# Two-axis attention block on one core: output products moved next to the projections, and one sum product in the time attention

## The chip, the cores and the metric

The kernel runs on one core of one Trainium2 chip. The metric is the device time of one launch in microseconds (us). The core has five engines with a queue each: PE (TensorE, matrix products into PSUM), ACT (ScalarE), DVE (VectorE), POOL (GpSimd) and SP (SyncE, which issues the large DMAs here). Each takes its instructions in the program's order; waits between engines go over semaphores.

## The reference

The input x is [2, 256, 128, 128] in f32: batch, time, frequency band, channel. Three residual blocks follow each other:

```
x = x + attention over time(layernorm(x))    # 4 heads of 32, causal, for each batch and band: 256 steps
x = x + attention over bands(layernorm(x))   # 4 heads of 32, |i - j| <= 16, for each batch and time: 128 bands
x = x + w2(gelu(w1(layernorm(x))))           # 128 -> 512 -> 128
```

Each attention is softmax(q k / sqrt(32) + mask) v, followed by an output projection. All of it is computed in f32.

## The kernel before

The kernel first folds scales and biases into the weights (`fold`), tests on the chip that the scores are bounded, and then takes `bounded_path`: since scores are bounded, softmax needs no maximum, so the weights are just exp of the scores, and masks set weights to zero afterwards.

The work is cut into groups of 4 tiles of 128 tokens x 128 channels. 128 `OverTime` groups come first (one group: two bands of 256 steps); their result goes to DRAM. Then 16 runs follow, each of 8 `OverBands` groups (4 time steps of 128 bands each) and the 8 `FeedForward` groups on the same tokens.

A group goes through these methods; each names what it puts on which engine:

- `statistics` (DVE), `root` (POOL: two instructions on rstd), `normalize` (DVE: xh), `transpose` (PE: xp), `take_transposed` (copies xp to xnT; DVE for `OverTime`, ACT for the others);
- `queries_keys` and `values` (PE: qp, kp, vp), `take_query` (ACT: qT), `take_key` (kT: DVE for `OverTime`, ACT for `OverBands`), `take_values` (ACT: v);
- scores (PE: sp) in `first_half` and, for `OverTime`, `second_half`; exp on ACT in `first_function` and `second_function` (pt, or pf for bands); masks in `first_mask` and `second_mask` (POOL; the last head or two of a band group on DVE, a product with `band`);
- `weigh` (PE: rp, the sums of the weights, each a product with ones; and op, the weights with v), `invert` (ACT: ln, then exp(-ln), r), `divide` (DVE: t, u, oT, where t reads rp and u reads op);
- `output` (PE: yp) and `finish` (DVE: adds yp to the residual; for `OverTime` two store DMAs on SP). `bias` (POOL) prepares the residual tile with the output bias (rd for time, x for bands, res for the feed-forward).

For `FeedForward` the two halves are the hidden products hp with their gelu (hT), `weigh` is the product zp, and `divide` adds and stores.

In the time attention a group's weights lie in a tile pt of [128, 2 sequences s, 4 heads, blocks of 128]. The keys are on the partitions. Block 0 holds the first 128 keys for the first 128 queries, block 1 the first keys for the second queries, block 2 the second keys for the second queries. POOL masks blocks 0 and 2 (the diagonal ones). The sum for the first queries is over block 0, the sum for the second over blocks 1 and 2, so `weigh` has two sum products for each head: one of 512 columns over blocks 0 and 1 of both sequences, one of 256 over block 2, which is added in PSUM.

What each product uses of PE's array stands in the profile's rows: sp uses 32 rows (a head's channels are contracted), rp and op use 32 columns (a head's channels come out), all others the whole 128 by 128.

All PSUM tiles are one bank in size and come from one pool of 8 (`bank`), in turn: a tile waits until the readers of the one eight before it are done. In SBUF, pt and pf share a tag with three buffers.

The order on each engine is that in which `run` calls the methods: a step n handles group n's scores while n - 1 is weighed, n - 2 is put out and n + 1 to n + 3 are prepared. `InOrder` pins each instruction to this order. `feeds[i]` and `bands[i]` tell whether group n - 2 + i is a `FeedForward` or an `OverBands`; an `OverTime` group is neither. As all instructions are recorded in that helper, the profile gives nearly all of them its line, L812 (L821 with the change), and they are told apart by their tiles.

Of the kernel before, what the change touches and what calls it, by code (L numbers as in the profile page):

```python
# [18 lines left out]
P = 128  # L19
H = 4  # L20
# [404 lines left out]
class Group:  # L425
# [48 lines left out]
    def take_transposed(self):  # L474
        path = self.path
        self.xnT = path.work.tile([P, NT * P], F32, name="xnT")
        if isinstance(self, OverTime):
            path.vector.tensor_copy(self.xnT, self.xp)
        else:
            path.scalar.copy(self.xnT, self.xp)  # L480

    def first_half(self):
        pass
# [13 lines left out]
    def second_mask(self):  # L497
        pass
# [16 lines left out]
    def weigh(self):  # L515
        pass
# [89 lines left out]
def rows_of(h):  # L606
    return slice(h * D, (h + 1) * D)


class OverTime(Attention):  # L610

    which = 0
# [22 lines left out]
    def weights(self, s):  # L637
        path = self.path
        for h in range(H):
            path.scalar.activation(self.p[:, s, h, :], self.sp[h], AF.Exp)  # L640

    def mask(self, s):
        path = self.path
        for n in (0, 2):
            blk = self.p[:, s, :, n * P : (n + 1) * P]
            path.gpsimd.affine_select(
                out=blk, in_=blk, compare_op=ALU.is_ge, fill=path.zero, base=0,
                pattern=[[0, H], [1, P]], channel_multiplier=-1,
            )

    def first_half(self):
        self.p = self.path.work.tile([P, 2, H, self.W], F32, name="pt", tag="p")
        self.scores(0)
# [4 lines left out]
    def first_mask(self):  # L658
        self.mask(0)

# [8 lines left out]

    def weigh(self):  # L670
# [3 lines left out]
        one = path.k.ones[:, 0:D]  # L674
        for h in range(H):
            path.tensor.matmul(rp[rows_of(h), :, :], one, p[:, :, h, 0 : 2 * P], start=True, stop=False)
        for h in range(H):
            path.tensor.matmul(rp[rows_of(h), :, P : 2 * P], one, p[:, :, h, 2 * P : W], start=False, stop=True)
# [14 lines left out]
class OverBands(Attention):  # L693
# [39 lines left out]
    def first_half(self):  # L733
        self.p = self.path.work.tile([P, H, NT, P], F32, name="pf", tag="p")
        self.scores(range(H))
# [81 lines left out]
class BoundedPath:  # L817
# [79 lines left out]
    def run(self, x, out):  # L897
# [7 lines left out]
        def at(n, kind):  # L905
            return 0 <= n < len(groups) and isinstance(groups[n], kind)

        self.scalar.preload_act_table_set(EXP_SET)
        for n in range(-10, len(groups) + 2):
# [7 lines left out]
            if feeds[1]:  # L917
                if bands[0]:
                    do(n - 2, "output", "finish")
                do(n - 1, "weigh", "divide")  # L920
            elif feeds[2]:
                do(n - 1, "weigh", "invert", "divide")
            else:
                do(n - 2, "output", "finish")
            if feeds[3]:
                do(n + 1, "transpose", "take_transposed")
            do(n + 2, "normalize")
            do(n + 3, "root")
            if not bands[2]:
                do(n, "bias")  # L930
                if at(n + RUN // NT, OverBands):
                    do(n + RUN // NT, "bias")
            if bands[2]:
                do(n, "second_mask")
            if not feeds[1] and not feeds[2]:
                do(n - 1, "weigh", "invert", "divide")
            do(n, "second_half", "second_function")
            if not bands[2]:
                do(n, "second_mask")
            if feeds[2] and bands[1]:  # L940
                do(n - 2, "output", "finish")
            do(n + 1, "queries_keys", "take_query", "take_key", "values", "take_values")
            if at(n + 2, Attention):
                do(n + 2, "transpose", "take_transposed")
# [69 lines left out]
```

## Time and profile before

| | before |
|---|---|
| time, median of 3 runs | 3059.23 us (3058.98 to 3059.82) |
| profiled execution: its time | 3059.68 us |
| profiled execution: span from the first to the last instruction | 3057.8 us |
| busy, PE / DVE / ACT / POOL | 99% / 68% / 64% / 58% of the span |
| matrix passes on PE | 31270 |
| first time step's scores on PE | 33.6 us from the start |
| first feed-forward product | 1210.9 us from the start |

In a row of the timeline stand start and length in us, engine, line, operation, output tile, operands, shape and how many were merged; in brackets the idle time before and who ended it. On PE the pair ahead of the shape (32*128) is rows times columns of the array. A length on PE is modelled and overlaps the next product's, so what a product costs is read from start to start. A row of the groups has count, busy time, mean length in ns, idle time ahead. A row of the waits has the total, the count and the longest.

### The profile page before, as it was taken

Reading aid. Unit: us, or ns where it says so; the run is one execution under the profiler, and the core shown is the slowest. Engines: PE = TensorE matmul, PEld = TensorE weight load, DVE = VectorE, ACT = ScalarE, POOL = GpSimd, SP = SyncE. Lnnn points to the kernel's source line nnn. Section 1 sums busy time; section 2 is a strip of 40 time slices with the busy share of each in tenths; the row PEclk is TensorE's granted clock in tenths of the full one; section 3 lists DMA queues with packets and bytes.
Section 4 is the critical chain, followed back from the end, with each engine's and each line's share of the span. In section 5 each row is a group of like instructions: output and inputs, shape, how many; then the busy total and the mean of one; then the engine's idle time right before and its main releaser. Section 6 shows DMA issues by size and latency. Waiting matters only on the chain.

```text
span 3057.8 us, 77275 instructions
## 1 busy us (share of the span) xinstructions
PE 3027.1 (99%) x31270; PEld 2134.0 (70%) x31270; DVE 2090.3 (68%) x6206; ACT 1960.3 (64%) x3536; POOL 1787.2 (58%) x2409
## 2 busy tenths in 40 slices
PE   7999999999999999999999999999999999999999
PEld 5666666666666666777777767777767767777776
DVE  6888788788888888467476475575575674664763
ACT  4666666666666667567566576576575675675664
POOL 3555555555555576566566566565565665665662
PEclk9999999999999999999999999999999999999999
DMA  3222222222222221111101011111111111011001
GB/s 83 60 60 57 65 69 58 59 60 60 70 61 60 57 60 54 42 32 40 43 29 43 29 39 38 34 39 36 36 39 39 32 40 42 29 43 39 15 19 29
DMA packets 222863, 140.53 MB, mean 46 GB/s; under 512 B 7968, under 2 KB 205984, under 8 KB 222496
## 3 DMA queue, kind: packets, MB, share of 16 engines
q1 hardware_dynamic: 221248, 134.45, 15.4%
q8 instruction: 247, 4.05, 0.5%
q10 hardware_dynamic: 1248, 1.05, 0.1%
q14 instruction: 120, 0.98, 0.1%
HBM read 68.36 MB, written 67.11 MB: 44 GB/s over the span
## 4 chain that ended last, share of the span: by engine, by line
PE 95%; DVE 3%; ACT 2%; DMA 0%; POOL 0%; issue 0%; SPq 0%; ACTq 0%; POOLq 0%; DVEq 0%
PE zp L812 15%; PE hp L812 13%; PE sp L812 12%; PE rp L812 9%; PE qp L812 9%; PE yp L812 8%; PE op L812 8%; PE vp L812 7%; PE kp L812 7%; PE xp L812 5%; DVE xh L812 1%; ACT L812 1%; DVE pf L812 0%; ACT r L812 0%; DVE stats L812 0%; ACT ln L812 0%
## 5 line engine op out<-in xcount | busy, mean ns | idle before, releaser
L812 POOL TENSOR_SCALAR_AFFINE_SELECT pf<-pf 128x512 f32<-128x512 f32 x736 | 499.0, 693 | 309.6 <-ACT pf L812 284.5
L812 POOL TENSOR_SCALAR_AFFINE_SELECT pt<-pt 128x512 f32<-128x512 f32 x512 | 313.5, 635 | 469.7 <-ACT pt L812 469.7
L812 ACT ACTIVATE pt<-sp 128x384 f32<-128x384 f32 x1024 | 419.5, 497 | 204.4 <-PE sp L812 204.4
L812 PEld LDWEIGHTS zp<-w2T_sb,hT 128*128 128x128 f32 x4096 | 475.2, 192 | 48.4 <-issue 46.3
L812 DVE TENSOR_TENSOR res<-zp,res 128x512 f32<-128x512 f32 x128 | 88.6, 692 | 583.8 <-POOL x L812 330.7
L812 PE MATMUL zp<-w2T_sb,hT 128*128 128x128 f32 x4096 | 479.9, 276 | 0.1
L812 PE MATMUL hp<-xnT,w1f 128*128 128x512 f32 x1024 | 471.8, 596 | 7.0 <-ACT xnT L812 7.0
L812 ACT ACTIVATE hT<-hp,b 128x512 f32<-128x512 f32 x512 | 344.8, 687 | 138.3 <-PE hp L812 135.9
L812 POOL TENSOR_TENSOR rstd<-rstd,mhalf 128x4 f32<-128x4 f32 x384 | 407.5, 1061 | 32.0
L812 PE MATMUL sp<-qT,kT 32*128 32x128 f32 (+1 forms) x8192 | 389.5, 315 | 0.0
L812 PEld LDWEIGHTS sp<-qT,kT 32*128 32x128 f32 x8192 | 311.1, 185 | 72.7 <-issue 40.4
L812 PEld LDWEIGHTS vp<-wf,xnT 128*128 128x128 f32 x2048 | 269.9, 192 | 122.8 <-issue 115.2
L812 ACT COPY xnT<-xp 128x512 f32<-128x512 f32 x256 | 150.5, 588 | 317.4 <-PE xp L812 317.4
L812 POOL TENSOR_SCALAR rstd<-mv 128x4 f32<-128x4 f32 x384 | 93.6, 244 | 410.6 <-DVE mv L812 410.6
L812 PEld LDWEIGHTS hp<-xnT,w1f 128*128 128x128 f32 x1024 | 181.0, 190 | 174.2 <-issue 134.5
L812 ACT ACTIVATE pf<-sp 128x512 f32<-128x512 f32 x512 | 264.3, 603 | 57.9 <-PE sp L812 50.4
L812 PE MATMUL yp<-wn,oT 128*128 128x128 f32 x2048 | 293.3, 286 | 0.0
L812 PE MATMUL qp<-xnT,wf 128*128 128x512 f32 x512 | 286.1, 641 | 0.8 <-DVE xnT L812 0.8
L812 PEld LDWEIGHTS yp<-wn,oT 128*128 128x128 f32 x2048 | 250.1, 191 | 42.7 <-PE hp L812 11.9
L812 PE MATMUL vp<-wf,xnT 128*128 128x128 f32 x2048 | 270.8, 276 | 0.0
L812 PE MATMUL kp<-xnT,wf 128*128 128x512 f32 x512 | 262.5, 594 | 0.0
L812 PE MATMUL xp<-ident,xh 128*128 128x128 f32 x1536 | 232.2, 274 | 10.1 <-DVE xh L812 10.1
(93 smaller groups left out, 4801.2 us busy)
## 6 DMA issues: line engine op xcount, KB each, us to landing
xt<-in_x SPq DMA_DIRECT2D x64, 512.0 KB, 5.1
x<-rd SPq DMA_DIRECT2D x256, 128.0 KB, 1.9
out<-res SPq DMA_DIRECT2D x128, 256.0 KB, 2.3
xb<-x SPq DMA_DIRECT2D x32, 0.5 KB, 6.1
w1T_sb<-in_w1T ACTq DMA_DIRECT2D x1, 256.0 KB, 4.0
w2T_sb<-in_w2T ACTq DMA_DIRECT2D x1, 256.0 KB, 4.4
t_wiT_sb<-in_t_wiT ACTq DMA_DIRECT2D x1, 192.0 KB, 2.5
f_wiT_sb<-in_f_wiT ACTq DMA_DIRECT2D x1, 192.0 KB, 3.8
```

Source lines behind the costliest of these rows:

```text
L812: return self.tc.keep_in_program_order(emit(*args, **kwargs))
```

## The change

It has four parts.

1. **One sum product in the time attention.** pt gets a fourth block for each sequence and head. Block 3 is blocks 1 + 2, added by POOL for the first sequence (behind the first masks) and by DVE for the second (a new method `last_sum`, at the end of the step). The sum product then reads blocks 0 and 3 of both sequences, 512 columns in four stretches of 128; the second sum product of each head is gone. op's products stay. Block 2 is masked ahead of block 0.
2. **Buffers.** pt and pf have two buffers instead of three.
3. **xnT on ACT.** `take_transposed` copies on ACT for all groups.
4. **The order of `run`.** `output` and `finish` move behind `weigh` (bands) or behind `second_half` (time), so that yp stands directly ahead of qp. Masks, `bias`, `normalize`, `root` and the transpose of the feed-forward groups move as shown.

```diff
--- before.py
+++ after.py
@@ -474,10 +474,7 @@
     def take_transposed(self):
         path = self.path
         self.xnT = path.work.tile([P, NT * P], F32, name="xnT")
-        if isinstance(self, OverTime):
-            path.vector.tensor_copy(self.xnT, self.xp)
-        else:
-            path.scalar.copy(self.xnT, self.xp)
+        path.scalar.copy(self.xnT, self.xp)

     def first_half(self):
         pass
@@ -495,6 +492,9 @@
         pass

     def second_mask(self):
+        pass
+
+    def last_sum(self):
         pass

     def queries_keys(self):
@@ -637,19 +638,25 @@
     def weights(self, s):
         path = self.path
         for h in range(H):
-            path.scalar.activation(self.p[:, s, h, :], self.sp[h], AF.Exp)
+            path.scalar.activation(self.p[:, s, h, 0 : self.W], self.sp[h], AF.Exp)

     def mask(self, s):
         path = self.path
-        for n in (0, 2):
-            blk = self.p[:, s, :, n * P : (n + 1) * P]
+        for n in (2, 0):
+            blk = self.block(s, n)
             path.gpsimd.affine_select(
                 out=blk, in_=blk, compare_op=ALU.is_ge, fill=path.zero, base=0,
                 pattern=[[0, H], [1, P]], channel_multiplier=-1,
             )

+    def block(self, s, n):
+        return self.p[:, s, :, n * P : (n + 1) * P]
+
+    def add(self, engine, s):
+        engine.tensor_tensor(self.block(s, 3), self.block(s, 1), self.block(s, 2), ALU.add)
+
     def first_half(self):
-        self.p = self.path.work.tile([P, 2, H, self.W], F32, name="pt", tag="p")
+        self.p = self.path.work.tile([P, 2, H, self.W + P], F32, name="pt", tag="p", bufs=2)
         self.scores(0)

     def first_function(self):
@@ -657,6 +664,7 @@

     def first_mask(self):
         self.mask(0)
+        self.add(self.path.gpsimd, 0)

     def second_half(self):
         self.scores(1)
@@ -667,15 +675,16 @@
     def second_mask(self):
         self.mask(1)

+    def last_sum(self):
+        self.add(self.path.vector, 1)
+
     def weigh(self):
         path = self.path
         p, v, W = self.p, self.v, self.W
         rp = path.bank([P, 2, 2 * P], "rp")
-        one = path.k.ones[:, 0:D]
+        sums = p.rearrange("p s h (n q) -> p s h n q", q=P)[:, :, :, 0:4:3, :]
         for h in range(H):
-            path.tensor.matmul(rp[rows_of(h), :, :], one, p[:, :, h, 0 : 2 * P], start=True, stop=False)
-        for h in range(H):
-            path.tensor.matmul(rp[rows_of(h), :, P : 2 * P], one, p[:, :, h, 2 * P : W], start=False, stop=True)
+            path.tensor.matmul(rp[rows_of(h), :, :], path.k.ones[:, 0:D], sums[:, :, h], start=True, stop=True)
         op = path.bank([P, 2, 2 * P], "op")
         for s in range(2):
             for h in range(H):
@@ -731,7 +740,7 @@
         path.scalar.copy(self.kT, self.kp)

     def first_half(self):
-        self.p = self.path.work.tile([P, H, NT, P], F32, name="pf", tag="p")
+        self.p = self.path.work.tile([P, H, NT, P], F32, name="pf", tag="p", bufs=2)
         self.scores(range(H))

     def weigh(self):
@@ -914,32 +923,28 @@
             if bands[2] and feeds[1]:
                 self.scalar.preload_act_table_set(EXP_SET)
             do(n, "first_half", "first_function", "first_mask")
-            if feeds[1]:
-                if bands[0]:
-                    do(n - 2, "output", "finish")
-                do(n - 1, "weigh", "divide")
-            elif feeds[2]:
-                do(n - 1, "weigh", "invert", "divide")
-            else:
-                do(n - 2, "output", "finish")
-            if feeds[3]:
-                do(n + 1, "transpose", "take_transposed")
             do(n + 2, "normalize")
             do(n + 3, "root")
+            if bands[2]:
+                do(n, "second_mask")
+            if feeds[2] and feeds[3]:
+                do(n + 1, "transpose", "take_transposed")
+            do(n - 1, "weigh")
+            if not feeds[1]:
+                do(n - 1, "invert")
+            if bands[2]:
+                do(n - 2, "output", "finish")
+            do(n - 1, "divide")
+            if feeds[3] and not feeds[2]:
+                do(n + 1, "transpose", "take_transposed")
+            do(n, "second_half", "second_function")
             if not bands[2]:
-                do(n, "bias")
+                do(n, "second_mask", "bias")
                 if at(n + RUN // NT, OverBands):
                     do(n + RUN // NT, "bias")
-            if bands[2]:
-                do(n, "second_mask")
-            if not feeds[1] and not feeds[2]:
-                do(n - 1, "weigh", "invert", "divide")
-            do(n, "second_half", "second_function")
-            if not bands[2]:
-                do(n, "second_mask")
-            if feeds[2] and bands[1]:
                 do(n - 2, "output", "finish")
             do(n + 1, "queries_keys", "take_query", "take_key", "values", "take_values")
+            do(n, "last_sum")
             if at(n + 2, Attention):
                 do(n + 2, "transpose", "take_transposed")
```

What this does to PE in the time stage, from a step's first scores to its query projection (sp are scores, yp the output product, rp sums, op weights with v, qp the projection; kp, vp and xp follow it in both). Before:

```order
L812 MATMUL sp<-qT,kT 128x256 x4
L812 MATMUL sp<-qT,kT 128x128 x4
L812 MATMUL yp<-wn_106,oT 128x128 x4
L812 MATMUL rp<-pt,ones 32x512 x4
L812 MATMUL rp<-pt,ones 32x2x128 x4
L812 MATMUL op<-pt,v 32x256 x4
L812 MATMUL op<-pt,v 32x128 x4
L812 MATMUL op<-pt,v 32x256 x4
L812 MATMUL op<-pt,v 32x128 x4
L812 MATMUL sp<-qT,kT 128x256 x4
L812 MATMUL sp<-qT,kT 128x128 x4
L812 MATMUL qp<-xnT,wf_103 128x512
```

With the change:

```order
L821 MATMUL sp<-qT,kT 128x256 x4
L821 MATMUL sp<-qT,kT 128x128 x4
L821 MATMUL rp<-pt,ones 32x512 x4
L821 MATMUL op<-pt,v 32x256 x4
L821 MATMUL op<-pt,v 32x128 x4
L821 MATMUL op<-pt,v 32x256 x4
L821 MATMUL op<-pt,v 32x128 x4
L821 MATMUL sp<-qT,kT 128x256 x4
L821 MATMUL sp<-qT,kT 128x128 x4
L821 MATMUL yp<-wn_106,oT 128x128 x4
L821 MATMUL qp<-xnT,wf_103 128x512
```

The product yp went from between sp and rp to between the step's second sp and qp, and the second row of rp is gone.

DVE in a step of the time stage, before (t, u and oT are the division, xh the normalized tile):

```order
L812 COPY xnT<-xp 128x512
L812 BN_STATS stats<-xt 128x6 x4
L812 BN_AGGR mv<-stats 128x2 x4
L812 TENSOR_TENSOR rd<-yp,rd 128x512
L812 TENSOR_SCALAR xh<-xt,mv,rstd 128x128 x4
L812 TENSOR_TENSOR t<-rp,r_14821 128x512
L812 TENSOR_TENSOR u<-op,r_14821 128x512
L812 SCALAR_TENSOR_TENSOR oT<-t,u 128x512
L812 COPY kT<-kp 128x512
```

With the change:

```order
L821 TENSOR_TENSOR pt<-pt 128x4x128
L821 BN_STATS stats<-xt 128x6 x4
L821 BN_AGGR mv<-stats 128x2 x4
L821 TENSOR_SCALAR xh<-xt,mv,rstd 128x128 x4
L821 TENSOR_TENSOR t<-rp,r_14702 128x512
L821 TENSOR_TENSOR u<-op,r_14702 128x512
L821 SCALAR_TENSOR_TENSOR oT<-t,u 128x512
L821 TENSOR_TENSOR rd<-yp,rd 128x512
L821 COPY kT<-kp 128x512
```

The copy of xnT is gone, the add on pt has come behind kT's copy, and rd<-yp has moved from ahead of xh to behind oT.

POOL in a step of the time stage, before and then with the change (the x4 are the second half's two masks and the next step's first two):

```order
L812 AFFINE_SELECT pt<-pt 128x4x128 x4
L812 TENSOR_SCALAR rstd<-mv 128x4
L812 TENSOR_TENSOR rstd<-rstd,mhalf 128x4
L812 TENSOR_TENSOR rd<-xt,orow_112 128x512
L812 AFFINE_SELECT pt<-pt 128x4x128 x4
```

```order
L821 AFFINE_SELECT pt<-pt 128x4x128 x2
L821 TENSOR_TENSOR pt<-pt 128x4x128
L821 TENSOR_SCALAR rstd<-mv 128x4
L821 TENSOR_TENSOR rstd<-rstd,mhalf 128x4
L821 AFFINE_SELECT pt<-pt 128x4x128 x2
L821 TENSOR_TENSOR rd<-xt,orow_112 128x512
```

The add on pt stands ahead of rstd, and rd's add has moved from between rstd and the second half's masks to behind them.

PE at the start of the feed-forward groups of a run, before (the first hp belongs to the first of them):

```order
L812 MATMUL sp<-qT,kT 128x128 x16
L812 MATMUL yp<-wn_146,oT 128x128 x4
L812 MATMUL xp<-ident,xh 128x128 x4
L812 MATMUL rp<-pf,ones 32x512 x4
L812 MATMUL op<-pf,v 32x128 x16
L812 MATMUL hp<-xnT,w1f 128x512 x2
L812 MATMUL rp<-pf,ones 32x512 x4
L812 MATMUL op<-pf,v 32x128 x16
L812 MATMUL xp<-ident,xh 128x128 x4
L812 MATMUL hp<-xnT,w1f 128x512 x2
L812 MATMUL yp<-wn_146,oT 128x128 x4
L812 MATMUL hp<-xnT,w1f 128x512 x2
```

With the change:

```order
L821 MATMUL sp<-qT,kT 128x128 x16
L821 MATMUL rp<-pf,ones 32x512 x4
L821 MATMUL op<-pf,v 32x128 x16
L821 MATMUL yp<-wn_146,oT 128x128 x4
L821 MATMUL xp<-ident,xh 128x128 x4
L821 MATMUL hp<-xnT,w1f 128x512 x2
L821 MATMUL xp<-ident,xh 128x128 x4
L821 MATMUL rp<-pf,ones 32x512 x4
L821 MATMUL op<-pf,v 32x128 x16
L821 MATMUL hp<-xnT,w1f 128x512 x2
L821 MATMUL yp<-wn_146,oT 128x128 x4
L821 MATMUL hp<-xnT,w1f 128x512 x2
```

The first xp is now directly ahead of its hp, and the second xp stands ahead of rp and not behind the second op.

## Prediction

> **What bounds the kernel now.** I read the page first, for its busy shares and its chain, then the list of waits, for those on PE.
>
> ```profile
> PE 3027.1 (99%) x31270; PEld 2134.0 (70%) x31270; DVE 2090.3 (68%) x6206; ACT 1960.3 (64%) x3536; POOL 1787.2 (58%) x2409
> ...
> PE 95%; DVE 3%; ACT 2%; DMA 0%; POOL 0%; issue 0%; SPq 0%; ACTq 0%; POOLq 0%; DVEq 0%
> ```
>
> ```profile
> PE hp L812 <- ACT xnT L812: 7.0, 16, 0.5
> ...
> PE rp L812 <- POOL pt L812: 1.3, 1, 1.3
> ```
>
> PE is the bound: it is 95% of the chain that ends last, and in the steady part it waits for another engine only 16 times (the first row of waits, once in each run of 8 band groups and 8 feed-forward groups). So what leaves PE's queue leaves the time, unless another engine takes its place. A busy PE says nothing of what a product costs, since products overlap; the starts do. Here is one step of the time stage on PE (start, length, product; the multiplicity is twice that of the code, as each f32 product shows as two passes):
>
> ```profile
> 803.36 0.94 PE L812 MATMUL sp<-qT,kT 32*128 32x256 f32 x16
> 804.22 1.16 PE L812 MATMUL yp<-wn,oT 128*128 128x128 f32 x8
> 805.31 1.50 PE L812 MATMUL rp<-pt,ones 128*32 128x512 f32 x16
> 806.62 1.48 PE L812 MATMUL op<-pt,v 128*32 128x256 f32 x32
> 808.04 0.94 PE L812 MATMUL sp<-qT,kT 32*128 32x256 f32 x16
> 808.90 1.13 PE L812 MATMUL qp<-xnT,wf 128*128 128x512 f32 x2
> 809.86 1.02 PE L812 MATMUL kp<-xnT,wf 128*128 128x512 f32 x2
> 810.72 1.05 PE L812 MATMUL vp<-wf,xnT 128*128 128x128 f32 x8
> 811.61 0.60 PE L812 MATMUL xp<-ident,xh 128*128 128x128 f32 x4
> 812.14 0.50 PE L812 MATMUL sp<-qT,kT 32*128 32x256 f32 x4
> ```
>
> From start to start a step takes 812.14 - 803.36 = 8.78 us, without a gap. The pair behind PE is the part of the array used: sp uses 32 rows, rp and op 32 columns, the others all of it. The same products with other neighbours:
>
> ```profile
> 1807.28 1.88 PE L812 MATMUL hp<-xnT,w1f 128*128 128x512 f32 x4
> 1808.99 1.05 PE L812 MATMUL yp<-wn,oT 128*128 128x128 f32 x8
> 1810.47 1.99 PE L812 MATMUL hp<-xnT,w1f 128*128 128x512 f32 x4 [0.42 <-ACT xnT L812]
> 1812.29 1.05 PE L812 MATMUL yp<-wn,oT 128*128 128x128 f32 x8
> 1813.18 2.06 PE L812 MATMUL zp<-w2T_sb,hT 128*128 128x128 f32 x17
> ```
>
> ```profile
> 1871.49 1.02 PE L812 MATMUL qp<-xnT,wf 128*128 128x512 f32 x2
> 1872.35 1.02 PE L812 MATMUL kp<-xnT,wf 128*128 128x512 f32 x2
> ...
> 1874.63 1.17 PE L812 MATMUL sp<-qT,kT 32*128 32x128 f32 x32
> 1875.73 1.06 PE L812 MATMUL rp<-pf,ones 128*32 128x512 f32 x8
> 1876.62 1.06 PE L812 MATMUL op<-pf,v 128*32 128x128 f32 x32
> 1877.60 1.13 PE L812 MATMUL qp<-xnT,wf 128*128 128x512 f32 x2
> ```
>
> yp alone between sp and rp takes 1.09 us (804.22 to 805.31); between hp and zp, which use the whole array as it does, 0.89 (1812.29 to 1813.18). So a stretch of whole-array products costs 0.20 for being a stretch: qp shows half of it at the entry, 0.96 behind sp (808.90) and 0.86 behind zp (1871.49). And the band stage's sums, one product of 512 columns for each head, take 0.89 directly behind sp (1875.73), against 1.31 for the time stage's two (805.31 to 806.62).
>
> **The change, part by part.** *Sums.* Each of 128 time groups loses the second sum product of each head, two passes of 256 columns. They take as long as one pass of 512, 0.43 (kp: 0.86 for two), so 1.31 becomes 0.88, the band stage's 0.89 to the rounding; 128 x 0.43 = 55.0 us. The one that is left reads blocks 0 and 3, four stretches of 128 instead of two of 256. No row has that. It can't be cheaper than one read straight; at the dear end it costs what four passes of 128 cost, 4 x 0.111 (vp: 0.89 for 8) against 0.43, twice a step: 0.03 a step, 4 us in all. I take 0, because the two sums with and without breaks (pt and pf) now have equal passes.
>
> *Order on PE.* The order lists show 497 whole-array stretches before and 273 after: 127 fewer in the time stage, where yp now stands ahead of qp, and 97 in the band stage, where it goes behind op and ahead of qp. 224 x 0.20 = 44.8 us. sp and op keep a neighbour of another kind on both sides, so they stay. A time step becomes 0.86 + 0.88 + 1.42 + 0.86 + 0.99 (yp with the entry) + 0.86 + 0.86 + 0.89 + 0.53 = 8.15 us. In the feed-forward steps only xp goes ahead of zp, whole array among whole array: 0.
>
> *What must now be ready sooner in a time step.* These rows carry it (ACT in a time step and, the fourth, in a band step; POOL; DVE; then a group of ACT; last the time stage's window, with its length and the busy time of PE, weight loads, DVE, ACT and POOL):
>
> ```profile
> 804.37 1.64 ACT L812 ACTIVATE pt<-sp 128x384 f32<-128x384 f32 x4 [0.76 <-PE sp L812]
> 806.90 0.60 ACT L812 ACTIVATE ln<-rp 128x512 f32<-128x512 f32 x1 [0.89 <-PE rp L812]
> 807.53 0.63 ACT L812 ACTIVATE r<-ln 128x512 f32<-128x512 f32 x1
> ```
>
> ```profile
> 1799.75 2.06 ACT L812 ACTIVATE pf<-sp 128x512 f32<-128x512 f32 x4 [0.56 <-PE sp L812]
> ```
>
> ```profile
> 806.08 1.22 POOL L812 TENSOR_SCALAR_AFFINE_SELECT pt<-pt 128x512 f32<-128x512 f32 x2 [2.94 <-ACT pt L812]
> 807.27 0.23 POOL L812 TENSOR_SCALAR rstd<-mv 128x4 f32<-128x4 f32 x1
> 807.58 1.04 POOL L812 TENSOR_TENSOR rstd<-rstd,mhalf 128x4 f32<-128x4 f32 x1
> 808.60 1.27 POOL L812 TENSOR_TENSOR rd<-xt,orow 128x512 f32<-128x512 f32 x1
> ```
>
> ```profile
> 809.51 0.91 DVE L812 SCALAR_TENSOR_TENSOR oT<-t,u 128x512 f32<-128x512 f32 x1
> 810.92 0.69 DVE L812 COPY kT<-kp 128x512 f32<-128x512 f32 x1 [0.50 <-PE kp L812]
> ```
>
> ```profile
> L812 ACT COPY xnT<-xp 128x512 f32<-128x512 f32 x256 | 150.5, 588 | 317.4 <-PE xp L812 317.4
> ```
>
> ```profile
> 60.00:1130.00 1070.00, 1070.00 (x12669) 724.76 (x12662) 860.21 (x2191) 689.36 (x1462) 609.75 (x858) 1.00 0.22 62
> ```
>
> Let S be the start of a step's first sp. ACT: the first weights run from S + 1.01 to S + 2.65 (804.37 and its 1.64, against 803.36). The copy of xnT that comes to ACT (0.59) follows v's, which is as long and starts 0.2 behind vp's end at S - 0.53: v ends near S + 0.26 and xnT near S + 0.85, 0.16 ahead of the weights. Late by some tenths it would push POOL's chain by as much; ACT is busy 689.36 / 1070.00 x 8.78 = 5.7 of a step now and 6.3 of 8.15 then. The copy's reader, qp, comes four us later. POOL: selects S + 2.72 to 3.94; the new add, priced as rd's, 1.27, to 5.19; rstd (0.31 + 1.04) to 6.5; the second half's selects, blocks 2 and 0, to 7.13 and 7.72; rd's add from 7.69 to 8.96. Its busy time goes from 5.0 to 6.3. The add has two full operands and rd's repeats one, so its price is an estimate between 1.27 and the longest two-input POOL row:
>
> ```profile
> L812 POOL TENSOR_TENSOR x<-xb,orow 128x512 f32<-128x512 f32 x1 | 1.7, 1718 | 0.0
> ```
>
> Even 1.72 moves DVE's add by 0.45 at most. DVE: it loses xnT's copy and gains the second add, both about 0.69 as kT's copy is, so its step stays at 860.21 / 1070.00 x 8.78 = 7.1 of now 8.15. kT starts 0.20 behind kp's end (810.92 against 810.72), so at S + 6.94, and DVE is free for the add at some S + 7.55 (0.08 ahead of its end, as its instructions overlap a little). Block 2 is masked by then (7.13); POOL is in block 0's select. The next step's rp is due at 8.15 + 0.86 = S + 9.01. Whether the add meets that turns on two lengths: oT beside rd above takes 0.91 and ends 0.55 behind it, and alone, in the band stage, 0.69:
>
> ```profile
> 1791.38 0.69 DVE L812 SCALAR_TENSOR_TENSOR oT<-t,u 128x512 f32<-128x512 f32 x1
> ```
>
> ```profile
> L812 POOL TENSOR_SCALAR_AFFINE_SELECT pf<-pf 128x512 f32<-128x512 f32 x1 | 1.1, 1103 | 0.1
> ```
>
> So DVE's instruction with two operands in SBUF waits out the POOL instruction in front of it, and POOL's next is the one that grows (a select of 1.10 behind DVE's pf product, 0.61 in the rows above). The add, there since 7.55, would go behind the select and ahead of rd's add: done at 7.72 + 0.55 = 8.27, 0.74 ahead of rp. Nothing shows on PE; rd's add ends by S' + 1.3, well before the next select at S' + 2.72. The Trainium skill, "SBUF — State Buffer", section "Who interferes with whom", has a rule against this change: a DVE instruction with two SBUF inputs and a GpSimd instruction that reads SBUF exclude each other for the whole of whichever started first. By it and rd's add in front, the sum would be the first rival's; with the select in front, it stays mine. The trace agrees with it in 0.91 against 0.69.
>
> *PSUM.* Of the 8 banks, kp now takes the one that rp had, and t is its last reader: r ends near S + 3.9 (weights to 2.65, then ln and r), t, as long as kT's copy, at 4.6; kp is due at S + 5.88. In the band stage, whose step becomes 1.10 + 0.89 + 0.98 + 0.99 + 0.86 + 0.86 + 0.89 + 0.53 = 7.10, the second sp of a step takes rp's bank: DVE's mask follows the weights at S + 3.3, then x<-yp, t, u and oT at 0.6 to 0.7 each, so t is done by S + 5.4, in time. *Output.* finish takes its two store DMAs along on SP, past nothing but loads issued ten groups ahead; on DVE it goes behind oT, ends near S + 6.6 and keeps clear of kT. rd has five buffers and is used for two more steps: hidden.
>
> *Start of the feed-forward groups.* Before, the first xp has rp and op behind it; now hp follows at once. With T the start of the last band group's sp, xp ends at T + 1.10 + 0.89 + 0.98 (op, 1876.62 to 1877.60) + 0.99 + 4 x 0.111 = 4.4. ACT has the weights done by T + 1.10 + 0.15 + 2.06 = 3.3 and ln and r by 4.55, and copies xnT until 5.1; hp starts at about 5.15: a wait of 0.75. The old wait goes (yp to hp 1.48 instead of 0.89, and hp behind it 1.82 instead of 1.71: 0.70), since the second xp is now far ahead. With the same 0.11 behind it the new one costs 0.86: 16 x 0.16 = 2.6 us lost.
>
> *First step.* PE's wait of 1.3 for the first masks gets one POOL add longer: 1.3.
>
> Sum: 55.0 + 44.8 - 2.6 - 1.3 = 95.9 us. The profiled execution took 3059.68 us, 1.9 more than its span, and the median is 3059.23: 3059.2 - 95.9 = 2963.3, say 2963. All other edits (loop order of the masks, two p buffers of larger size, whose last reader op stands a step ahead of the next writer) I cost at nothing.
>
> **The rivals.** *A: DVE's add falls behind rd's add.* If kp is only 0.14 later against POOL, the add reaches its turn after 7.69 and waits for rd's end, 8.96, ending at 9.51, so rp waits 0.50 and some 0.05 for the signal. A wait x of rp delays kp by x in that step, which keeps the add behind, and gives the next step x back: x' = 0.55 - x, 0.28 a step on average. 127 x 0.28 = 35 us: 2998. For it: the margin is 0.14 in a chain of ten terms. Against: a later POOL widens it, and waits outside 0.14 to 0.41 fall back to 0.
>
> *B: the stretches' 0.20 is not the array's shape but fresh operands.* Then yp keeps its 1.09: only the sums go, 3059 - 55 + 4 = 3008. Against: yp and qp, with the same operands, have both values.
>
> *C: slower, by POOL.* If the add with two full operands takes y, block 2 is masked at 7.13 + (y - 1.27) and rp is ready 1.21 later; the step becomes 7.48 + (y - 1.27), over 8.78 from y = 2.57, and past the band stage's gain (97 x 0.20 - 2.6 = 17 us, 0.13 a step) from y = 2.70. At 3.0 the step is 9.21: 3059 + 127 x 0.43 - 17 = 3097. Against: no POOL instruction of that size takes more than 1.72.
>
> *D: the change does not reach PE*, because another wait of 0.6 a step (a bank, a buffer of p) takes what is freed: 3059 - 17 = 3042 or less. The rows show none.
>
> **How the numbers follow.** The forecast has 0.73, A 0.14, B 0.05, C 0.03, D 0.05. The range goes from 2956 (small terms of 7 us that I counted as lost or left out) to 3002, past A and the 4 us of the strided read. What a measurement of this kernel can tell from no change is 0.2%, 6 us. Faster 0.95, same 0.02, slower 0.03.
>
> **What would show it.** Right: on PE a time step of 8.15 us, rp 0.88, yp 0.99, and in the list of waits only hp for xnT, 16 times at about 0.75. A shows as PE's rp waiting for DVE's pt, with pt's add over 1 us long. B: yp at 1.09. C: the POOL add's own length. D: a new row in PE's waits. I am wrong if PE's starts in the time stage stay 8.5 us apart or more.

## The result, and the profile after

The changed kernel takes 2968.59 us (median of 4 runs, 2968.23 to 2968.87), the kernel before, on the same chip, 3059.48 (3058.98 to 3059.82): a ratio of 0.9703, 95% interval 0.9686 to 0.972. It is 90.9 us faster where 95.9 were forecast. The profiled execution took 2968.23 us with a span of 2966.3.

From the page of the changed kernel, the busy shares and the chain:

```profile
PE 2929.6 (99%) x30246; PEld 2082.9 (70%) x30246; DVE 1933.7 (65%) x6206; ACT 2007.6 (68%) x3664; POOL 2057.4 (69%) x2537
...
PE 99%; ACT 0%; DMA 0%; DVE 0%; POOL 0%; issue 0%; SPq 0%; ACTq 0%; POOLq 0%; DVEq 0%
```

PE is still the bound and now nearly all of the chain (99% instead of 95%). It has 1024 passes fewer, the 128 x 8 of the second sum products. POOL's load went from 1787.2 to 2057.4 us, and no engine took PE's place. The list of waits on PE:

```profile
PE hp L821 <- ACT xnT L821: 10.8, 16, 0.7
PE xp L821 <- DVE xh L821: 10.6, 1, 10.6
...
PE rp L821 <- DVE pt L821: 2.5, 1, 2.5
```

Only the first row is paid in every run; the other two stand once, at the start. One step of the time stage on PE:

```profile
799.77 0.94 PE L821 MATMUL sp<-qT,kT 32*128 32x256 f32 x16
800.63 1.07 PE L821 MATMUL rp<-pt,ones 128*32 128x512 f32 x8
801.51 1.48 PE L821 MATMUL op<-pt,v 128*32 128x256 f32 x32
802.93 0.94 PE L821 MATMUL sp<-qT,kT 32*128 32x256 f32 x16
803.79 1.16 PE L821 MATMUL yp<-wn,oT 128*128 128x128 f32 x8
804.79 1.02 PE L821 MATMUL qp<-xnT,wf 128*128 128x512 f32 x2
805.65 1.02 PE L821 MATMUL kp<-xnT,wf 128*128 128x512 f32 x2
806.51 1.05 PE L821 MATMUL vp<-wf,xnT 128*128 128x128 f32 x8
807.40 0.60 PE L821 MATMUL xp<-ident,xh 128*128 128x128 f32 x4
807.93 0.50 PE L821 MATMUL sp<-qT,kT 32*128 32x256 f32 x4
```

807.93 - 799.77 = 8.16 us instead of 8.78, without a gap. rp takes 0.88, yp with the entry 1.00, qp behind it 0.86. The same step on POOL and DVE, where the added instructions are:

```profile
803.67 1.28 POOL L821 TENSOR_TENSOR pt<-pt 128x512 f32<-128x512 f32 x1
...
804.90 0.23 POOL L821 TENSOR_SCALAR rstd<-mv 128x4 f32<-128x4 f32 x1
804.91 0.73 DVE L821 SCALAR_TENSOR_TENSOR oT<-t,u 128x512 f32<-128x512 f32 x1
...
805.22 1.32 POOL L821 TENSOR_TENSOR rstd<-rstd,mhalf 128x4 f32<-128x4 f32 x1
...
806.52 1.22 POOL L821 TENSOR_SCALAR_AFFINE_SELECT pt<-pt 128x512 f32<-128x512 f32 x2
806.71 0.69 DVE L821 COPY kT<-kp 128x512 f32<-128x512 f32 x1 [0.47 <-PE kp L821]
...
807.32 0.97 DVE L821 TENSOR_TENSOR pt<-pt 128x512 f32<-128x512 f32 x1
...
807.71 1.71 POOL L821 TENSOR_TENSOR rd<-xt,orow 128x512 f32<-128x512 f32 x1
```

DVE's add starts 7.55 behind S (the start of the step's first scores, 799.77), the forecast's number to the hundredth. It waits for POOL's select, goes ahead of POOL's add of rd, and is done at S + 8.52, half a microsecond before the next rp at S + 9.02 (sp and rp above: 8.16 + 0.86). POOL's add of rd pays for it: 1.71 instead of 1.27.

The start of a run's feed-forward groups (PE and, in between, ACT):

```profile
1130.14 1.16 PE L821 MATMUL yp<-wn,oT 128*128 128x128 f32 x8
...
1131.14 0.60 PE L821 MATMUL xp<-ident,xh 128*128 128x128 f32 x4
1131.78 0.58 ACT L821 COPY xnT<-xp 128x512 f32<-128x512 f32 x1
1132.38 1.28 ACT L821 ACT_TABLE_LOAD   x1
...
1132.41 1.13 PE L821 MATMUL hp<-xnT,w1f 128*128 128x512 f32 x2 [0.67 <-ACT xnT L821]
```

From xp to hp 1.27 us pass where four passes of xp take 0.44: the new wait, 0.83 here. The first hp of the first run starts at 1132.4 us instead of 1210.9, 78.5 us sooner. Of this, 1.1 us lies ahead of the first time step's scores (32.5 us from the start instead of 33.6; 32.5 to 34.5 in the profiles of all runs below), so it is no part of the change; the rest is that of the time stage and the first run's band groups. From its first hp to that of the next, a run takes 117.57 us instead of 118.44, which over fifteen runs gives the other 13 of the 91.5 us by which the span fell.

### The profile page after: what moved, and what is told of

It reads as the page before. It is cut to its first block, busy times and chain, and to the rows that moved or that the text cites. A ratio compares the mean times of both kernels' runs of the same rounds, so it can differ in the third digit from the quotient of the medians.

```text
span 2966.3 us, 75357 instructions
## 1 busy us (share of the span) xinstructions
PE 2929.6 (99%) x30246; PEld 2082.9 (70%) x30246; DVE 1933.7 (65%) x6206; ACT 2007.6 (68%) x3664; POOL 2057.4 (69%) x2537
## 4 chain that ended last, share of the span: by engine, by line
PE 99%; ACT 0%; DMA 0%; DVE 0%; POOL 0%; issue 0%; SPq 0%; ACTq 0%; POOLq 0%; DVEq 0%
PE zp L821 16%; PE hp L821 15%; PE sp L821 12%; PE op L821 9%; PE yp L821 9%; PE rp L821 9%; PE vp L821 8%; PE qp L821 8%; PE kp L821 7%; PE xp L821 6%; ACT xnT L821 0%; DMA xt<-in_x 0%; DMA f_wiT_sb<-in_f_wiT 0%; POOL pt L821 0%; POOL rstd L821 0%
## 5 line engine op out<-in xcount | busy, mean ns | idle before, releaser
L821 POOL TENSOR_SCALAR_AFFINE_SELECT pf<-pf 128x512 f32<-128x512 f32 x736 | 508.2, 705 | 277.1 <-ACT pf L821 252.0
L821 POOL TENSOR_TENSOR rstd<-rstd,mhalf 128x4 f32<-128x4 f32 x384 | 460.6, 1200 | 32.0
L821 PEld LDWEIGHTS zp<-w2T_sb,hT 128*128 128x128 f32 x4096 | 469.0, 192 | 10.2 <-issue 8.1
L821 DVE TENSOR_TENSOR t<-rp,r 128x512 f32<-128x512 f32 x256 | 175.4, 685 | 215.0 <-ACT r L821 213.4
L821 ACT ACTIVATE pf<-sp 128x512 f32<-128x512 f32 x512 | 264.3, 603 | 57.2 <-POOL rstd L821 32.5
L821 DVE TENSOR_TENSOR pf<-pf,band 128x512 f32<-128x512 f32 x144 | 142.6, 999 | 214.4 <-ACT pf L821 214.4
L821 ACT COPY v<-vp 128x512 f32<-128x512 f32 x256 | 149.8, 585 | 173.9 <-PE vp L821 173.9
L821 PE MATMUL qp<-xnT,wf 128*128 128x512 f32 x512 | 265.0, 600 | 0.7 <-ACT xnT L821 0.7
```

What stands on the lines that cost most here:

```text
L821: return self.tc.keep_in_program_order(emit(*args, **kwargs))
```

## The experiments

The theory: the change's two gains are PE's own, 0.43 us a step from the sums and 0.20 from each whole-array stretch, and they are had because the adds on POOL and DVE stay ahead of rp, by an order in which DVE's two-operand instructions don't wait for POOL's long ones. The rivals: the stretches cost nothing in themselves (the forecast's B), DVE and POOL don't exclude each other, or the order matters only for PE.

**e1: the new order without the new sums.** Both adds go, and `weigh` has its two sum products back; all else as in the changed kernel.

```diff
-        self.add(self.path.gpsimd, 0)
-        self.add(self.path.vector, 1)
...
-            path.tensor.matmul(rp[rows_of(h), :, :], path.k.ones[:, 0:D], sums[:, :, h], start=True, stop=True)
+            path.tensor.matmul(rp[rows_of(h), :, :], one, p[:, :, h, 0 : 2 * P], start=True, stop=False)
+        for h in range(H):
+            path.tensor.matmul(rp[rows_of(h), :, P : 2 * P], one, p[:, :, h, 2 * P : W], start=False, stop=True)
```

> The new order of run, two p buffers and xnT on ACT are kept; the fourth block and both adds are taken away, and the two sum products of each head are back. My theory, by which the gain is two independent sums on PE: 128 x 0.43 us come back, so about 3023 us, a time step of 8.16 + 0.43 = 8.59 us and rp at 1.31 us. Rival, that the order alone gives nothing and all of the gain is the lost product: about 3059 us. Rival, that the order gives all of it: about 2969 us.

Measured: 3020.39 us, ratio 0.9871 (0.9855 to 0.9886). The time step is 8.592 us, 0.196 less than before's 8.788, with no gap on PE in either, and a run of 16 groups is as long as in the changed kernel (117.57 us). So the order by itself is worth 39 us, and B falls: a stretch costs 0.20 when the sums are untouched. The sums make the rest, 3020.4 - 2968.6 = 51.8: 127 x (8.592 - 8.161) = 54.7, less 3.1 in the first step.

**e2: the new sums in the old order.** The kernel before, with the fourth block, both adds and the one sum product; xnT of the time stage is copied by DVE as before. The two p buffers and the new order of the masks come with them; the cut shows only the place of DVE's add.

```diff
             do(n + 1, "queries_keys", "take_query", "take_key", "values", "take_values")
+            do(n, "last_sum")
```

> The order of run and the copy of xnT on DVE are those of before; only the fourth block, the two adds and the one sum product are new. My theory: only 128 x 0.43 us go, and the first step loses about 2 us: about 3006 us, a time step of 8.79 - 0.43 = 8.36 us, yp still at 1.09 us. DVE's add now waits for masks that stand behind rd's add on POOL, near 8.7 us after the step's start, and rp is due near 10.3, so it should hold. Rival, that the adds come too late without the new order: the step stays above 8.5 us and PE's rp waits for DVE's pt, 3025 us or more.

Measured: 3090.48 us, ratio 1.0101 (1.0085 to 1.0116): slower than before, where the expectation had it well below. PE does have less to do, but a step takes 9.0 us, and the list of PE's waits has a new first row, which is not the wait that the rival named (rp waits for DVE's pt only 9 times, 5.7 us in all):

```profile
PE sp L824 <- DVE kT L824: 68.7, 119, 0.9
```

DVE and then POOL in a step and a half of e2:

```profile
805.61 1.54 DVE L824 SCALAR_TENSOR_TENSOR oT<-t,u 128x512 f32<-128x512 f32 x1
807.07 0.68 DVE L824 COPY kT<-kp 128x512 f32<-128x512 f32 x1
...
810.93 2.44 DVE L824 TENSOR_SCALAR xh<-xt,mv,rstd 128x128 f32<-128x128 f32 x4
```

```profile
805.33 1.26 POOL L824 TENSOR_TENSOR rd<-xt,orow 128x512 f32<-128x512 f32 x1
...
810.57 1.22 POOL L824 TENSOR_SCALAR_AFFINE_SELECT pt<-pt 128x512 f32<-128x512 f32 x2 [2.34 <-ACT pt L824]
811.76 1.27 POOL L824 TENSOR_TENSOR pt<-pt 128x512 f32<-128x512 f32 x1
```

oT, 0.69 when alone, is issued 0.28 behind POOL's add of rd and takes 1.54: it ends 0.56 behind that add. xh, 1.08 in the changed kernel where POOL is idle beside nearly all of it, takes 2.44 beside POOL's selects and its new add. So kT is written late, and the next scores wait. Two readings were left: DVE is simply full (its instructions stand back to back), or a chain runs through these two meetings.

**e8: e2 with the copy of xnT on ACT.** It takes 0.6 us of work from DVE.

```diff
-        if isinstance(self, OverTime):
-            path.vector.tensor_copy(self.xnT, self.xp)
-        else:
-            path.scalar.copy(self.xnT, self.xp)
+        path.scalar.copy(self.xnT, self.xp)
```

> The run with the sums alone, in the order of before, but with xnT's copy on ACT. There DVE was busy through all of a 9.0 us step, 1.5 of it in oT (0.7 alone) and 2.4 in xh (1.1 alone). Theory, that DVE with its waits for POOL is what bound that run: taking 0.60 us off DVE takes 0.60 off the step, 8.40 us, near PE's 8.36: about 3013 us. Rival, that a chain of waits through kT bound it and not DVE's sum: 3060 us or more. Rival, that the waits for POOL fall away as well once DVE has room: 3006 us, PE's own step.

Measured: 3091.87 us, ratio 1.0104 (1.0088 to 1.0119), the same as e2, with the same wait (70.2 us, 119 times). The theory that DVE's sum bounds e2 falls. With the copy gone, xh starts sooner against POOL's selects and just takes longer, 2.81: the room goes into the wait.

**e9: e2 with POOL's add of rd behind the second half's masks.** Nothing is removed; one instruction of POOL changes its place, away from oT.

```diff
-            if not bands[2]:
-                do(n, "bias")
...
-                do(n, "second_mask")
+                do(n, "second_mask", "bias")
```

> The sums in the order of before (e2), with one edit: in the time stage POOL's add of rd goes behind the second half's masks. Theory (e2's step of 9.0 us is a chain through DVE, not DVE's sum: oT takes 1.54 us since it waits for POOL's add of rd, so kT is written 0.85 late, and the next scores wait 0.57 for it): oT takes about 0.7, kT follows kp at once, the step falls to PE's own 8.36 to 8.40 and the time to 3090.5 - 127 x 0.62 = 3012 us (3007 to 3020). Rival (the other meeting, xh at 2.4 us beside POOL's masks and add, is enough by itself, or DVE waits elsewhere): the step stays over 8.7 us and the time over 3050.

**e10: e8 with xh ahead of the add of yp on DVE.** Here xh is moved away from POOL's selects, and rd's add on POOL stays where it was.

```diff
             else:
+                do(n + 2, "normalize")
                 do(n - 2, "output", "finish")
```

> The sums in the order of before with xnT on ACT (e8), with one other edit: in the time stage and the band stage DVE's xh goes ahead of rd<-yp, so that two of its four instructions run before POOL's masks begin. Theory (the chain): xh ends some 1.5 us sooner (at 3.7 behind the step's first scores instead of 5.4), t follows r, oT is through before POOL's add of rd begins and takes 0.7, and the step is PE's 8.36 to 8.40: 3091.9 - 127 x 0.64 = 3011 us (3006 to 3020). Rival (oT still meets POOL's add of rd, or DVE's add of pt does, and one meeting is enough): the step stays over 8.7 us and the time over 3050.

Measured: e9 3009.3 us in three of its five executions, ratio 0.9835 (0.9815 to 0.9854); e10 3014.72, ratio 0.9854 (0.9837 to 0.987). Either move can take out the whole loss. In e10 the step is 8.356, which is PE's own (8.788 - 0.431), xh takes 1.40 and oT 0.69; eight odd steps of 9.0 and one of 8.65, seven of them at the end of the time stage where POOL has one more add (x of the first band groups), and a longer first step make most of the 5 to 6 us between the two. So e2's loss is a chain, scores, weights, POOL's masks and add, xh, t, u, oT, kT, scores. With xh's meeting alone it doesn't close (e11 below: xh takes 2.65, and the step is PE's), and in e10, where xh's is short, oT's meeting with rd's add doesn't come about.

e9's times came at two levels, at a granted clock of 0.999 or 1.0 in all: three executions at 3008.69 to 3009.3, and two at 3066.71 and 3067.14, one of them the one profiled, with steps of 8.836. In these two the move took out less than a third of the loss. The ratio is that of the three.

**e11: e9's kernel again, for a profile at the lower level.**

> The kernel of e9 once more, for a profile of an execution of 3009 us (the one profiled there took 3067, with steps of 8.836 us, oT 1.12, DVE's add of pt 1.75 and the next scores waiting 0.4 for kT). Theory: at 3009 a step is 8.36 us, oT takes 0.7, DVE's add of pt stands directly behind kT and is through before POOL's add of rd, and PE doesn't wait for kT; the two kinds of execution differ only in which of DVE's add and POOL's add of rd is first. Rival: at 3009 oT still takes over 1 us, and the time came back elsewhere.

Measured: 3008.5 us, ratio 0.9831 (0.9803 to 0.986), steps of 8.356, but four of the last five 8.84 to 8.90. So one execution holds both orders. A step in the middle, and then one of those four (POOL, DVE and PE by time):

```profile
804.10 2.65 DVE L824 TENSOR_SCALAR xh<-xt,mv,rstd 128x128 f32<-128x128 f32 x4
...
807.99 0.69 DVE L824 SCALAR_TENSOR_TENSOR oT<-t,u 128x512 f32<-128x512 f32 x1
808.15 1.61 POOL L824 TENSOR_SCALAR_AFFINE_SELECT pt<-pt 128x512 f32<-128x512 f32 x2 [0.41 <-ACT pt L824]
...
809.21 1.10 DVE L824 TENSOR_TENSOR pt<-pt 128x512 f32<-128x512 f32 x1
...
809.74 1.71 POOL L824 TENSOR_TENSOR rd<-xt,orow 128x512 f32<-128x512 f32 x1
...
1076.08 1.67 POOL L824 TENSOR_SCALAR_AFFINE_SELECT pt<-pt 128x512 f32<-128x512 f32 x2 [0.45 <-ACT pt L824]
...
1076.14 1.12 DVE L824 SCALAR_TENSOR_TENSOR oT<-t,u 128x512 f32<-128x512 f32 x1
...
1077.72 1.26 POOL L824 TENSOR_TENSOR rd<-xt,orow 128x512 f32<-128x512 f32 x1
1077.78 1.75 DVE L824 TENSOR_TENSOR pt<-pt 128x512 f32<-128x512 f32 x1
...
1078.00 0.94 PE L824 MATMUL sp<-qT,kT 32*128 32x256 f32 x16 [0.41 <-DVE kT L824]
```

In the first, xh takes 2.65 beside POOL's masks and add without a loss; oT starts 0.16 ahead of the select and takes 0.69; DVE's add of pt then goes ahead of POOL's add of rd (1.10 and 1.71). In the second, oT starts 0.06 behind the select and takes 1.12, the add of pt comes behind rd's (1.75 and 1.26), and PE waits 0.41 for kT. Which of two instructions is first by a tenth of a microsecond is worth 0.48 us a step, and each order makes itself again in the next step: the theory of e11 holds. The trace shows where e11 goes from one to the other: from the step in which POOL first has one more add (x of the first band groups), oT's lead over the select falls from 0.18 to 0.09, then to 0.00, and then oT is 0.03 behind. In e9's profiled execution the select is in front from the second step on (by 0.09), long before any such add, and stays there. What decides it in the first steps was not tried.

**e3: the changed kernel with xnT of the time stage on DVE.** The third part of the change is undone alone.

```diff
-        path.scalar.copy(self.xnT, self.xp)
+        if isinstance(self, OverTime):
+            path.vector.tensor_copy(self.xnT, self.xp)
+        else:
+            path.scalar.copy(self.xnT, self.xp)
```

> The changed kernel with xnT of the time stage copied by DVE again, as before the change. My theory, that PE alone sets the step and this copy is hidden on either engine: within 3 us of 2968.6 us, step 8.16 us, with DVE busy some 7.7 us of it. Rival, that the copy had to leave DVE to make room for the add: the add or t comes late, PE waits at rp, over 2980 us.

Measured: 2973.69 us, ratio 0.972 (0.9707 to 0.9734), 5 us over the changed kernel. The step stays 8.161, and only six at the end of the time stage, where POOL has one more add (x of the first band groups), take 8.95 to 8.99:

```profile
PE sp L824 <- DVE kT L824: 3.2, 6, 0.6
```

6 x 0.8 = 4.8 us are nearly the whole difference. So 0.6 us of DVE's work is hidden in all other steps, and the move of xnT is no large part of the order's 39.

**e5: the changed kernel with one more DVE copy, of kp, ahead of DVE's add.** The add is thus 0.6 later, at the place where rd's add of POOL is in front.

```diff
     def last_sum(self):
+        more = self.path.work.tile([P, NT * P], F32, name="more", bufs=2)
+        self.path.vector.tensor_copy(more, self.path.late)
         self.add(self.path.vector, 1)
```

> The changed kernel with one more copy of kp by DVE (0.61 us, into a tile that nothing reads) between kT's copy and the add on pt, so that the add comes to its turn 8.16 us after the step's start and not 7.55, behind the start of rd's add on POOL (7.94). By the exclusive turn of DVE's two-operand instruction and POOL's, which the first rival of the prediction rests on: the add ends near 9.76, rp (due at 9.03) waits, 0.39 a step on average, about 3018 us; with DVE's lock waits added up over a full step, as in the run with the sums alone, up to 8.9 a step and 3065 us. Rival, no exclusion: the add ends at 8.85, in time, and the time stays within 4 us of 2968.6.

Measured: 3041.77 us, ratio 0.9941 (0.9925 to 0.9956): 73 us for a copy of 0.6. PE's waits, and the meeting in one step:

```profile
PE rp L824 <- DVE pt L824: 67.3, 127, 2.5
```

```profile
793.35 0.94 PE L824 MATMUL sp<-qT,kT 32*128 32x256 f32 x16
...
801.57 1.27 POOL L824 TENSOR_TENSOR rd<-xt,orow 128x512 f32<-128x512 f32 x1
...
801.89 1.50 DVE L824 TENSOR_TENSOR pt<-pt 128x512 f32<-128x512 f32 x1
...
803.54 1.07 PE L824 MATMUL rp<-pt,ones 128*32 128x512 f32 x8 [0.69 <-DVE pt L824]
```

The add, issued 0.32 behind rd's, ends 0.55 behind its end, and rp waits. Steps of about 8.55 and 8.93 alternate. This is the forecast's rival A, made on purpose: the wait comes as A described it, a wait in one step and less in the next, because kp is delayed by it too. Its size, 0.58 a step, is above the 0.39 expected and A's 0.28: rd's add itself starts 8.22 behind the step's first scores (801.57 against 793.35), where A had 7.69, because POOL and DVE meet elsewhere too (xh takes up to 2.79, and POOL's first instruction on rstd 0.71 behind oT instead of 0.23). In A's terms, 0.55 + 0.53 shared by two steps makes 0.54 a step. DVE and POOL do exclude each other here: an add of 0.69 that is issued 0.6 later would end at S + 8.84, ahead of rp's S + 9.02, and the copy would have cost nothing.

**e6: the changed kernel with the second add on POOL too**, behind the second half's masks.

```diff
     def second_mask(self):
         self.mask(1)
+        self.add(self.path.gpsimd, 1)

     def last_sum(self):
-        self.add(self.path.vector, 1)
+        pass
```

> The changed kernel with the second sequence's add on POOL too, behind the second half's masks and ahead of rd's add; DVE has none. Theory, that what counts is when rp's last operand is ready: the masks end 7.97 after the step's start, the add 1.27 later at 9.2, rp is due at 9.03, so 0.25 a step: 8.41 us and about 3000 us, with rp waiting for POOL's pt. Rival, that only an engine's busy share counts (POOL 7.6 of 8.16): within 4 us of 2968.6. Rival, that POOL's instructions take longer than their rows: over 3020 us.

Measured: 2991.03 us, ratio 0.9776 (0.9761 to 0.9791), 22 us over the changed kernel. POOL's add ends just behind the moment at which rp is due:

```profile
813.15 1.26 POOL L822 TENSOR_TENSOR pt<-pt 128x512 f32<-128x512 f32 x1
813.44 0.94 PE L822 MATMUL sp<-qT,kT 32*128 32x256 f32 x16
...
814.47 1.06 PE L822 MATMUL rp<-pt,ones 128*32 128x512 f32 x8
```

rp is due 0.86 behind sp, at 814.30, the add ends at 814.41, and rp starts at 814.47; the steps alternate around 8.29, 0.13 over 8.161. The sign was as expected, the size a step half of it, since a wait in one step again shortens that of the next. Another 5.5 of the 22 us are six steps of 9.08 to 9.10 at the end of the time stage, where POOL has the add of x besides. The split of the two adds over two engines is thus worth 22 us.

**e4: the changed kernel with the transpose of a run's first feed-forward group a step earlier**, behind vp. It takes away the wait that the forecast costed as lost.

```diff
-            if feeds[3] and not feeds[2]:
-                do(n + 1, "transpose", "take_transposed")
...
-            if at(n + 2, Attention):
+            if at(n + 2, Attention) or (feeds[4] and not feeds[3]):
                 do(n + 2, "transpose", "take_transposed")
```

> The changed kernel, but the transpose of a run's first feed-forward group goes to the end of the step before, directly behind vp, where the band groups have theirs. My theory: the 16 waits of hp for xnT go, each 0.84 us ahead of hp and 0.10 in its first pass, as xnT is then ready three products ahead: 16 x 0.94 = 15 us, so about 2954 us, and no wait for xnT in PE's list. Rival, that the wait only moves (to a bank, to the gelu's table load or to the second hp): 2963 us or more with a new row in PE's waits.

Measured: 2960.64 us, ratio 0.9677 (0.9664 to 0.969), 8.0 less than the changed kernel and half of what was expected. The wait for xnT is gone from the list, but the first zp of a run now takes 4.05 us instead of 3.57: it waits for its gelu, behind the table loads that ACT needs between ln, exp and gelu.

**e7: e4 with one table load fewer in each run.** ACT loads the table set that holds exp and ln ahead of the last band group's ln, so that ln and exp share it.

```diff
+            if feeds[2] and bands[1]:
+                self.scalar.preload_act_table_set(EXP_SET)
```

> The kernel with the early transpose, and ahead of the ln of a run's last band group one table load of the set that holds both exp and ln, so that ACT loads two tables there and not three. Theory: in the run with the early transpose half of the gain was lost since the first zp (4.05 us instead of 3.57) now waits for the gelu behind these loads; 1.28 us earlier on ACT frees it: 16 x 0.47 = 7.6 us, about 2953 us. Rival, that zp waits for something else (a bank, or the DVE division behind r): 2958 us or more, zp still at 4.0 us.

Measured: 2952.74 us, ratio 0.965 (0.9637 to 0.9663), faster than the changed kernel (0.9703, 0.9686 to 0.972). A run takes 116.621 us, in e4 117.096. The rows of the groups for the table loads, of e4 and of e7:

```profile
L821 ACT ACT_TABLE_LOAD x80 | 102.6, 1283 | 18.3 <-DVE flag L421 16.9
```

```profile
L821 ACT ACT_TABLE_LOAD x64 | 82.1, 1283 | 18.1 <-DVE flag L421 17.0
```

Sixteen loads of 1.28 us are gone, and 7.9 of their 20.5 us were on PE's path.

## Why the prediction was right, point by point

- **PE is the bound and stays it**: right, 99% of the chain.
- **Sums, 0.43 a step and 55.0 in all**: right. rp takes 0.88, so reading four stretches of 128 costs nothing; e1 beside the changed kernel gives 0.431.
- **Order, 0.20 a stretch**: right, 0.196 a step in e1, also where yp and qp were predicted singly (1.00 and 0.86 against 0.99 and 0.86).
- **DVE's add ahead of rd's add on POOL**: right in mechanism and issue (S + 7.55); its end is S + 8.52, not 8.27. POOL is late by a quarter: the second instruction on rstd takes 1.32 instead of 1.04, and it starts 0.31 behind oT, which is still running. This is the same exclusion with the engines' parts exchanged: in e3's time steps that instruction takes 1.32 to 1.38 where oT has started before it and still runs (82 times), and 1.04 in the other 45; in e1, where oT comes behind it, it takes 1.04. A later POOL widens the margin for DVE's turn, as the forecast said, from 0.14 to 0.39 (807.71 against 807.32); that the unforeseen meeting fell on POOL's side, and not on DVE's, was luck. e5 shows what the other turn costs. The Trainium skill, "SBUF — State Buffer", section "Who interferes with whom", has the pair exclude each other for the whole of whichever started first; the runs agree (e5: the add ends 0.55 behind rd's end; e11: 1.10 or 1.75 by who was first).
- **First step, 1.3 lost**: too small. It takes 11.555 us instead of 9.056, 2.5 lost although a sum of 0.43 is saved there too, as PE waits there for DVE's add and not only for POOL's: a first step has no lead over the chain.
- **Start of the feed-forward groups, 0.16 a run lost**: right in mechanism, but 0.25. The new wait is 0.94 with the slower hp behind it (0.86 forecast), because the copy of xnT starts 0.64 behind xp's start (1131.78), where ACT's own end had been taken as the last event; the old one that went was 0.69 (0.70). Besides, xp behind op paid only 0.05 of entry before, so half of a stretch's entry there was no gain.
- **The sum**: 95.9 against 90.9 by the medians, and 91.5 by the two spans, of which 90.4 lie behind the first scores. Of the 5.5 us missing there, the first step makes 1.6 (2.5 lost, where 1.3 less the sum of 0.43 makes 0.9), the run starts 16 x (0.09 + 0.05) = 2.2, stretches of 0.197 for 0.200 make 0.7, the last two time steps (8.26) 0.2; some 0.8 stay unassigned.
- **The rivals**: A did not happen by a margin of some tenths, and e5 and e11 show that it is real. B is refuted by e1, C by the POOL add's 1.28 us, D by PE's waits.

One thing the forecast did not see: it added sums and order as if each stood alone. In the old order they don't. The order alone gives 39 us, the sums alone lose 31, both together give 91. In the old order the new adds close a chain over POOL and DVE, and the moves of xh and of rd's add, which the forecast took to be hidden, are what opens it (e9, e10). In the new order the terms do add up, because PE waits for neither add in a step; that much the forecast had worked out.

## What to carry to other kernels

Taking work off the bounding engine by giving it to two others is only worth its price if the receivers' instructions don't meet: look at the trace for instructions of DVE with two SBUF operands (and of the kind of xh) beside POOL's, and price each meeting at the rest of POOL's instruction plus most of their own length (0.55 of 0.69 here). An idle share of 30% on an engine says little when its instructions stand in a chain with another's; what decides is who is in front at each meeting, and the move of one instruction was worth 81 us of 3090 here. Look at the end of a stage too, where one engine already works for the next: in e3, e6, e10 and e11 the longer steps stand where POOL has one more add. Cost the first step and each hand-over between stages by itself, with the producer's end plus the hand-over, from the latest of all inputs.

## What the runs showed of the hardware that had not been expected

- Two self-keeping orders in one program: e9's kernel runs its steps at 8.356 or 8.836 us at an unchanged clock, and goes from one to the other within an execution, where POOL has one more add (e11).
- Relieving DVE of 0.6 us (e8) moved nothing, loading it with 0.6 ahead of stats (e3) cost 5 us, and ahead of the add (e5) 73: what DVE waits in its meetings with POOL depends on when it arrives, not on how much it has to do.
- xh, which reads one tile and two scalars for each row, is held up beside POOL as the two-tile instructions are: 1.08 us with POOL idle, 1.40 (e10), 2.44 (e2), 2.65 (e11) and 2.81 (e8) the more of it lies beside POOL's selects and add.
- A stretch's entry depends on the product that enters: behind the same op, xp pays 0.05 (before the change, 0.49 from start to start against 0.44) and yp 0.10 (with it, 0.99 against 0.89).
